# A four-layer kernel: layer 3's keys made inside the attention, its weights prepared in front of layer 2's end, three-step turns in layer 2, another order of sums and taps in layer 1

## Chip, cores and metric

The kernel runs on one core of a Trainium2 chip. The metric is device time in microseconds; lower is better. Engines are named as in the profile: PE (TensorE), PEld (its weight loads), DVE (VectorE), ACT (ScalarE), POOL (GpSimd), SP (SyncE, which issues all DMAs here).

## What is computed

The input x is 2x128x64x64 in float32 (2 batches, 128 channels, 4096 pixels). Four layers follow one another, each as a residual around a group norm:

```python
def _gn(v, G=32, eps=1e-5):           # mean and variance over groups of 4 channels
    ...
x = x + _L0_conv_ref(_gn(x), ...)     # 1x1 and 3x3 depthwise convolutions, two attentions over tokens and channels
x = x + _L1_conv_ref(_gn(x), ...)     # 1x3 convolution, correlations over shifts, 5x5 dilated depthwise taps
x = x + _L2_conv_ref(_gn(x), ...)     # rfft2, a quaternion product with weights per frequency, irfft2
x = x + _L3_conv_ref(_gn(x), ...)     # attention, 8 heads of 16 channels, 4096 queries and keys
```

In layer 3, q, k and v are 1x1 projections with a bias, the logits are divided by the root of 128, and softmax runs over all 4096 keys.

## The kernel before, in words

The whole x lies in SBUF as `X` (128 channels by 2 batches by 4096) and every layer adds to it in place. All loops are unrolled. Each layer is recorded under `_in_order`, which fixes every engine's order to the order of the program, so an instruction that waits holds what was written after it on its engine. DMAs are issued by SP in program order too. Pools of SBUF are opened and closed by layer, so a later layer's first load waits until the layer before has released its space.

*Layer 0* (`_layer0`): per batch `convolutions`, then `attention`, whose exps are ACT's L1294, scores PE's L1285, and products L1698. Before it, `_weights_by_rows` issues 136 DMAs (L764, L766) that rearrange layer 2's weights from HBM to HBM.

*Layer 1* (`_layer1`): loads its weights (L536 to L544); `padded` normalizes (L149); `columns_and_convolved` makes a convolution `t2` (L610) and transposed columns (L620); `correlated` multiplies columns (L635) and swaps the result (`swapped`, L646). Then come 42 taps of batch 0 on DVE (`taps`, L655), the matrices `t9` (`weights`, L693), and a loop over 2 batches and 8 chunks of 512 pixels (`NCH`). In each step, `on_tiles` (L674, for chunks 0 and 2, copied to `z` by ACT at L684) and `combined` (L703, 14 matmul instructions) run on PE; some taps of batch 1, a step of the next layer's statistics (`_stats_steps`: L1323, L1326, matmuls L1329 and L1338) and `added` (L714) run on DVE.

*Layer 2* (`_layer2`): first the transforms over h, 8 turns for each batch. `columns` normalizes on ACT (`g`, L832), transposes on PE (L839) and copies on DVE (`gt`, L845); `transformed` multiplies (L852) and copies on ACT (`y`, L853). `_skewed` runs `columns(i)` and then `transformed(i-1)`. Then come 8 blocks `kb` of two halves each. A half is `products` (L970) with weights loaded at L795, and beside it a chain of side steps, dealt out by `alongside`: `rows_in` transforms the rows of the next block (L874, ACT's L880, L887) and copies them into operands `e` (ACT's L910, DVE's L912); `turned` and `back` transform the results back (L999, L1006, L1024, L1027). In block 0 the first half also makes the mirrored operand of its own rows. At the end `turned_back` (L1091, L1099) and `added` (L1106, L1108) add to `X`.

*Layer 3* (`_layer3`): loads constants, weights and biases with 13 DMA issues (L104, L1870, L1874, L1876, L1878), prepares them (`weights`, L1887 to L1893), and folds the norm into them (`folded`, L1904 to L1923). `queries_and_keys` makes a batch's q and k in 8 chunks: a matmul (L1938), two shuffles on DVE (L1941, L1943), three scalings on ACT if `idle` (L1946 to L1948) or else on DVE, and two combinations on DVE (L1953, L1954). `values` makes `vt` in 8 groups (L1964, L1971). Both take their PSUM tiles from `acc`, which has two buffers; `attend` holds one of them as its accumulator. For each of 8 blocks `qb` and 32 tiles `kt`, `attend` makes scores (L2010), two exps (L2020) and, two tiles later, the products with `vt` (L2029). There are four such passes (2 batches, 2 halves of the heads). For the first pass, all 8 chunks and 2 groups of values are made ahead of it, and the other 6 groups inside it, one every third `kt`:

```python
                if kt % 3 == 0:
                    over = next(early, early) is early
```

For later passes all of this is side work of the pass before, one step at `kt` 4, 12 and 20, once `early` is over.

Of the kernel before, what the change touches and what calls it, by code (L numbers as in the profile page):

```python
# [520 lines left out]
def _layer1(ctx, tc, X, a, cst, here=None, there=None):  # L521
# [204 lines left out]
    rest = taps(1, g[1])  # L726
    steps = iter(())
    for b in range(B):
        for c in range(NCH):
            if c in (0, 2):  # L730
                z = on_tiles(g[b], t2[b], c // 2)
                some(rest, 4)
            ps = combined(t9[b], t2[b], c)
            some(rest, 2)
            some(steps, 2)
            added(b, c * CH, ps)
            if c in (1, 3):
                added(b, c // 2 * S // 2, z)
        if there is not None and b == 0:
            steps = _stats_steps(nc, two, bank, X[:, 0, :], cst, mhalf, there)  # L740


# [31 lines left out]
@with_exitstack  # L774
def _layer2(ctx, tc, X, weights, cst, src, here=None, there=None):

# [25 lines left out]
    with tc.tile_pool(name="l2_a", bufs=3) as ap, tc.tile_pool(  # L802
# [18 lines left out]
        for b in range(B):  # L821
# [7 lines left out]

            def columns(i):  # L830
                g = ap.tile([128, 8, H], F32, name="g")
                nc.scalar.activation(  # L832
                    g, xw[:, 8 * i : 8 * i + 8, :], AF.Identity, bias=shift, scale=scale
                )
                for _ in range(2):
                    next(steps, None)
                pt = aps.tile([128, CH], F32, tag="pt", name="ps_pt")
                for n in range(4):
                    nc.tensor.transpose(  # L839
                        pt[:, n * 128 : (n + 1) * 128],  # L840
                        g[:, 2 * n : 2 * n + 2, :].rearrange("p w h -> p (w h)"),
                        ident,
                    )
                gt = ap.tile([128, CH], F32, name="gt")
                nc.vector.tensor_copy(gt, pt)  # L845
                return gt
# [9 lines left out]

            _skewed(columns, transformed, W // 8)

    two = ctx.enter_context(tc.tile_pool(name="l2_two", bufs=2))
    with tc.tile_pool(name="l2_e", bufs=4) as ep, tc.tile_pool(  # L860
# [191 lines left out]
        for i in (0, 2):  # L1052
            for _ in rows_in(0, first[i : i + 2], (0,), es):
                pass
        before = None
        for kb in range(BLOCKS2):
# [7 lines left out]
            if before:  # L1064
                side += [turned(pzs[1], before[1]), back(kb - 1, *before)]
                n += 6
            else:
                side = [rows_in(0, first[i : i + 2], (1,), e) for i in (0, 2)] + side
                n += 10
            alongside(products(rows_of_weights(kb, False), e[0], pzs[0]), chain(*side), n)  # L1070
            side, n = [turned(pzs[0], direct)], 4
            if nxt:
                side = [rows_in(kb + 1, nxt[2:], (1, 0), es)] + side
                n += 8
            alongside(products(rows_of_weights(kb, True), e[1], pzs[1]), chain(*side), n)
            before = (direct, image)
        for _ in chain(turned(pzs[1], before[1]), back(BLOCKS2 - 1, *before)):
            pass


    with tc.tile_pool(name="l2_c", bufs=3) as cp, tc.tile_pool(
# [176 lines left out]
def _in_order(tc):  # L1258
# [4 lines left out]
    for i in block[start:]:  # L1263
        if i.engine in ENGINES:
            if i.engine in last:
# [7 lines left out]
                )  # L1273
            last[i.engine] = i.name


# [74 lines left out]
def _layer0(ctx, tc, X, a, cst, worst, there, dram):  # L1351
# [442 lines left out]
    for b in range(1, B):  # L1794
        _input(nc, X, a, b)
    rows_of_weights = _weights_by_rows(nc, dram, a)
    with _in_order(tc):
# [27 lines left out]
    for b in range(B):  # L1825
        w2 = small.tile([128, 128], F32, tag="w2", name="w2")
        with tc.tile_pool(name="f0_conv", bufs=1) as pool, _in_order(tc):
            ss2, own = convolutions(pool, b, before)
        side = [channel_attention(ss2, own, w2)]
        if b + 1 < B:  # L1830
# [7 lines left out]


@with_exitstack  # L1840
def _layer3(ctx, tc, X, a, cst, src, out, worst, here):
    nc = tc.nc
    SCALE = 1.0 / math.sqrt(C)
    OF_Q = [i % 16 for i in range(32)]
# [10 lines left out]

    k3 = _load_consts(nc, one, src, 2)

    upper, sign = k3["upper"], k3["sign"]
    lower = one.tile([128, 1], F32, name="lower")
    mhalf = one.tile([128, 1], F32, name="mhalf")  # L1860
    nc.vector.memset(mhalf, -0.5)
    head_sum = _all_ones_blocks(nc, one)


    w_qk = one.tile([128, 2, 4, 2, 16], F32, name="w_qk")
    b_qk = one.tile([128, 2], F32, name="b_qk")
    loaded = []
    for n, p in enumerate("qk"):
        w = two.tile([128, CH], F32, tag="ur"[n], name="w", bufs=1)[:, : 2 * 128]
        nc.sync.dma_start(w, a[f"L3_conv_w{p}"].rearrange("p t m -> p (t m)"))  # L1870
        loaded.append(w.rearrange("p (t j s i) -> p t j s i", t=2, s=2, i=16))
        for j in range(4):
            r = 32 * j + 16 * n
            nc.sync.dma_start(b_qk[r : r + 16, :], a[f"L3_conv_b{p}"][32 * j : 32 * j + 16, :])  # L1874
    w_v = one.tile([128, 192], F32, name="w_v")
    nc.sync.dma_start(w_v, a["L3_conv_wv"])  # L1876
    b_v = one.tile([128, 192], F32, name="b_v")
    nc.sync.dma_start(b_v, a["L3_conv_bv"].to_broadcast([128, 192]))  # L1878

    residual = [one.tile([128, CH], F32, name=f"residual{i}") for i in range(2)]  # L1880
    for r in residual:
        nc.gpsimd.memset(r, 0.0)

    def weights():
        for n, w in enumerate(loaded):
            for t in range(2):
                nc.vector.tensor_scalar_mul(  # L1887
                    w_qk[:, t, :, n, :], w[:, t, :, 0, :], SCALE if n == 0 else 1.0
                )
        nc.vector.tensor_scalar(lower, upper, -1.0, 1.0, ALU.mult, ALU.add)  # L1890
        scales = one.tile([128, 1], F32, name="scales")
        nc.vector.scalar_tensor_tensor(scales, lower, SCALE, upper, ALU.mult, ALU.add)
        nc.vector.tensor_scalar_mul(b_qk, b_qk, scales)  # L1893

# [32 lines left out]
    def queries_and_keys(b, t, f, q, k, idle):  # L1927
# [7 lines left out]
        for c in range(NCH):  # L1935
# [8 lines left out]
            hi = two.tile([128, CH], F32R, tag="hi", name="hi", bufs=1)  # L1944
            if idle:
                nc.scalar.activation(hi, kk, AF.Identity, bias=bk)  # L1946
# [55 lines left out]
    def attend(b, t, q, k, vt, early):  # L2002
# [58 lines left out]
        for qb in range(NCH):  # L2061
            for kt in range(NQT):
                if kt % 3 == 0:
                    over = next(early, early) is early
                waiting.append((qb, kt, scores(qb, kt)))
                if len(waiting) > 2:
                    multiply(*waiting.pop(0))
                yield kt if over else None
        for x in waiting:
            multiply(*x)  # L2070

    def work():

        for b in range(B):
            f = []
            yield from folded(b, f)
            for t in range(2):
# [4 lines left out]
                early = values(b, t, f, vt)  # L2082
                for n, _ in enumerate(early):
                    yield
                    if first and n == 1:
                        break
                yield from queries_and_keys(b, t, f, q, k, first)
                yield b, t, (q, k, vt, early)
# [9 lines left out]
    side = work()  # L2098

    next(side)  # L2100
    weights()
    found = []
# [45 lines left out]
def kernel(ctx, tc, a, out):  # L2148
# [4 lines left out]
    with tc.tile_pool(name="keep", bufs=1) as keep:  # L2153
# [4 lines left out]
        rows_of_weights = _layer0(tc, X, a, cst, worst, st[:, :B], dram)  # L2158
        _layer1(tc, X, a, cst, st[:, :B], st[:, B])
        _layer2(tc, X, rows_of_weights, cst, a["consts1"], st[:, B], st[:, B + 1])  # L2160
        _layer3(tc, X, a, cst, a["consts2"], out, worst, st[:, B + 1])
        with tc.tile_pool(name="flag_ps", bufs=1, space=PSUM) as fp:
# [68 lines left out]
```

## Time and profile before

| | |
|---|---|
| time, median of 3 runs | 4331.19 us (4329.97 to 4339.18) |
| the profiled execution's own time | 4336.11 us |
| its span, first to last instruction | 4334.3 us |
| PE, ACT, DVE, POOL busy | 94%, 77%, 50%, 2% of the span |
| granted PE clock, mean | 0.972 |
| layer 0, layer 1, layer 2, layer 3 | 0 to 1707.9, to 1965.7, to 2318.1, to 4334.3 us |

Most of the time is attention: layer 0's exps (L1294) occupy ACT for 992.5 us, layer 3's (L2020) for 1885.1 us. A busy PE in the profile isn't a PE at its peak, since the ends of matmuls are modelled. The stages between the attentions are shorter, and in each of them another engine or wait decides; they have to be read from their own windows. The profiled execution lies 4.9 us above the median.

### The profile page before, as it was taken

How to read it: one execution, taken by the hardware profiler on the slowest of the kernel's cores; microseconds unless marked ns; L12 is line 12 of the kernel's file. 1: busy time of each engine (PE TensorE's matmuls, PEld its weight loads, DVE VectorE, ACT ScalarE, POOL GpSimd, SP SyncE). 2: the span in 40 equal slices, each digit the busy share in tenths (PEclk: the TensorE clock that was granted, in tenths of full speed). 3: DMA queues.
4: the chain of work that ended last, by engine and by line, in shares of the span. 5: the costliest groups of instructions: out<-in, count | busy, mean ns of one | idle time of the engine just before them, and what ended most of it. 6: DMA issues, size and time to landing. Idle time of an engine off the chain costs nothing. (4 is left out here: it accounts for less than half of the span.)

```text
span 4334.3 us, 82274 instructions
## 1 busy us (share of the span) xinstructions
PE 4080.3 (94%) x35790; PEld 1559.5 (36%) x35790; DVE 2178.7 (50%) x2340; ACT 3353.9 (77%) x4069; POOL 67.5 (2%) x145
## 2 busy tenths in 40 slices
PE   6899999978999997996896999999999999999998
PEld 3432222245222224444664333333333333333332
DVE  3578999846999998994764112312122112211111
ACT  4378888734888884225553999999999999999998
POOL 1001000000000001000000000000000000000000
PEclk9999999989999999998997999999999999999999
DMA  9998000000000000002660000000000000000000
GB/s 206 187 182 115 1 1 1 1 1 2 1 1 1 1 1 7 1 1 114 260 273 8 4 6 6 6 4 6 6 6 4 6 6 6 4 6 6 6 6 4
DMA packets 158822, 158.86 MB, mean 37 GB/s; under 512 B 24809, under 2 KB 148713, under 8 KB 154354
## 3 DMA queue, kind: packets, MB, share of 16 engines
q1 hardware_dynamic: 158450, 153.50, 15.1%
q8 instruction: 282, 4.62, 0.4%
q14 instruction: 90, 0.74, 0.1%
HBM read 145.09 MB, written 73.40 MB: 50 GB/s over the span
## 5 line engine op out<-in xcount | busy, mean ns | idle before, releaser
L2020 ACT ACTIVATE weights<-ps_s 128x1024 f32<-128x1024 f32 x2048 | 1885.1, 1104 | 67.3 <-PE ps_s L2010 66.9
L1294 ACT ACTIVATE weights<-ps_s 128x1024 f32<-128x1024 f32 x1024 | 992.5, 1022 | 174.0 <-PE ps_s L1285 149.1
L2029 PE MATMUL ps_acc<-weights,vt 128*32 128x512 f32 x8192 | 1098.2, 608 | 0.0
L2010 PE MATMUL ps_s<-q,k 32*128 32x512 f32 x8192 | 929.4, 446 | 8.9 <-ACT weights L2020 8.9
L1733 DVE TENSOR_TENSOR sums<-sums,weights 128x2048 f32<-128x2048 f32 x384 | 879.0, 2289 | 42.1 <-ACT weights L1294 6.2
L2010 PEld LDWEIGHTS ps_s<-q,k 32*128 32x128 f32 x8192 | 474.8, 184 | 846.8 <-ACT weights L2020 785.1
L1285 PE MATMUL ps_s<-q,k 32*128 32x512 f32 x4096 | 645.8, 641 | 3.6 <-ACT weights L1294 2.2
L2051 DVE COPY u<-ps_acc 128x512 f32<-128x512 f32 x32 | 22.1, 691 | 1068.6 <-PE ps_acc L2029 1068.6
L1698 PE MATMUL ps_acc<-weights,vt 128*32 128x512 f32 x4096 | 548.9, 605 | 3.4 <-ACT used L1723 3.2
L1285 PEld LDWEIGHTS ps_s<-q,k 32*128 32x128 f32 x4096 | 209.6, 183 | 429.8 <-issue 212.5
L2029 PEld LDWEIGHTS ps_acc<-weights,vt 128*32 128x32 f32 x8192 | 163.4, 108 | 379.7 <-issue 367.8
L1698 PEld LDWEIGHTS ps_acc<-weights,vt 128*32 128x32 f32 x4096 | 81.0, 108 | 395.8 <-issue 377.7
L655 DVE SCALAR_TENSOR_TENSOR X<-g,w,X 128x2048 f32<-128x2048 f32 x84 | 197.3, 2350 | 2.4
L1489 PE MATMUL ps_sp<-pad,diag 32*32 32x512 f32 x4608 | 178.9, 633 | 9.8 <-DVE q L1500 5.5
L1733 DVE TENSOR_TENSOR sums<-weights 128x2048 f32<-128x2048 f32 x64 | 146.5, 2289 | 61.5 <-ACT weights L1294 61.5
L1971 DVE TENSOR_TENSOR vt<-ps_acc,bv 128x384 f32<-128x384 f32 x32 | 17.8, 557 | 294.3 <-PE ps_acc L1964 294.3
L970 PE MATMUL ps_z<-w_ri,e 128*32 128x128 f32 x2048 | 137.6, 408 | 8.8 <-DVE e L912 6.6
L1489 PEld LDWEIGHTS ps_sp<-pad,diag 32*32 32x32 f32 x4608 | 96.9, 106 | 79.5 <-issue 33.7
L1467 PE MATMUL ps_sp<-xn,w_qkv 128*128 128x512 f32 x160 | 88.6, 691 | 32.4 <-DVE k L1500 15.0
L2054 DVE RECIPROCAL r<-r 128x512 f32<-128x512 f32 x32 | 107.3, 3353 | 1.1
L912 DVE TENSOR_SCALAR e<-ps_pe 32x136 f32<-32x136 f32 (+1 forms) x352 | 104.4, 297 | 5.0
L910 ACT ACTIVATE e<-ps_pe 32x136 f32<-32x136 f32 (+1 forms) x352 | 99.2, 282 | 4.1
(285 smaller groups left out, 2514.1 us busy)
## 6 DMA issues: line engine op xcount, KB each, us to landing
w_ri<-w_r SPq DMA_DIRECT2D x16, 2112.0 KB, 8.2
w_ri<-w_i SPq DMA_DIRECT2D x16, 2112.0 KB, 13.4
w_r<-in_L_conv_kr_w SPq DMA_DIRECT2D x15, 528.0 KB, 13.1
w_r<-in_L_conv_kr_x SPq DMA_DIRECT2D x15, 528.0 KB, 12.8
w_r<-in_L_conv_kr_y SPq DMA_DIRECT2D x15, 528.0 KB, 12.7
w_r<-in_L_conv_kr_z SPq DMA_DIRECT2D x15, 528.0 KB, 12.6
w_i<-in_L_conv_ki_w SPq DMA_DIRECT2D x15, 528.0 KB, 12.7
w_i<-in_L_conv_ki_x SPq DMA_DIRECT2D x15, 528.0 KB, 12.1
```

Of the source, the lines that this page charges most:

```text
L655: nc.vector.scalar_tensor_tensor(xi, g[:, i : i + H // 2, j : j + W], w8[:, s : s + 1], xi, ALU.mult, ALU.add)
L912: nc.vector.tensor_scalar_mul(out, got[of, :, s], sign)
L970: nc.tensor.matmul(out.rearrange("p (n f o) -> p n f o", n=2, f=2), e[:, s, 2 * j : 2 * j + 2, :].rearrange("p f x -> p (f x)"), w.rearran ...
L1285: nc.tensor.matmul(ps[j // 2][:, j % 2, :], k[rows, kt * 128 : (kt + 1) * 128], q[rows, qb * CH : (qb + 1) * CH], start=True, stop=True,)
L1294: nc.scalar.activation(w[:, 2 * p : 2 * p + 2, :], ps[p], AF.Exp)
L1489: nc.tensor.matmul(ps[r // 2][to, r % 2, :].rearrange("p (h w) -> p h w", w=W), diag[rows, grp, t, :], pad[rows, y0 : y0 + ROWS, t % 3 : t ...
L1698: nc.tensor.matmul(ac[n][rows, :], lhs(rows), w[:, j, :], start=first, stop=last)
L1733: nc.vector.tensor_add(parts[0].rearrange("p j c -> p (j c)"), t.rearrange("p j c -> p (j c)"), w.rearrange("p j c -> p (j c)"),)
L2010: nc.tensor.matmul(ps[j // 2][:, j % 2, :], k[rows, kt * 128 : (kt + 1) * 128], q[n][rows, qb * CH : (qb + 1) * CH], start=(n == 0), stop= ...
L2020: nc.scalar.activation(w[p], ps[p], AF.Exp)
L2029: nc.tensor.matmul(ac[0][32 * j : 32 * j + 32, :], vt[:, kt, j // 2, i : i + 2, :].rearrange("p a d -> p (a d)"), w[j // 2][:, i, :], star ...
L2054: nc.vector.reciprocal(r, r)
```

## The change

Layer 3: the loads and the preparation of weights become functions of their own. The loads are issued ahead of layer 1, into two new pools; the preparation runs on DVE ahead of the last part of layer 2. The first pass begins after two chunks of keys (scaled on ACT) and two groups of values; the other six of each are made inside the pass, in turn, one every second `kt`, with the keys' scalings on DVE. Layer 2: the transforms over h take three steps per turn, with `transformed` two turns behind the normalization; in block 0, the rows of block 1 move from the first half to the second. Layer 1: a chunk's sum is written after the next chunk's `combined` and ahead of its taps, and the taps are dealt out 4 and 3 per step instead of 6 and 2. Layer 0: the DMAs of `_weights_by_rows` wait for the last instruction of batch 0's convolutions.

```diff
@@ _layer1
             if c in (0, 2):
                 z = on_tiles(g[b], t2[b], c // 2)
-                some(rest, 4)
             ps = combined(t9[b], t2[b], c)
-            some(rest, 2)
+            for x in ready:
+                added(*x)
+            ready = [(b, c * CH, ps)]
+            if c in (1, 3):
+                ready.append((b, c // 2 * S // 2, z))
+            some(rest, 4 if c in (0, 2) else 3)
             some(steps, 2)
-            added(b, c * CH, ps)
-            if c in (1, 3):
-                added(b, c // 2 * S // 2, z)
...
@@ _layer2
-            _skewed(columns, transformed, W // 8)
+            gs, gts = {}, {}
+            for i in range(W // 8 + 2):
+                if i < W // 8:
+                    gs[i] = normalized(i)
+                if 1 <= i <= W // 8:
+                    gts[i - 1] = columns(i - 1, gs.pop(i - 1))
+                if i >= 2:
+                    transformed(i - 2, gts.pop(i - 2))
...
             else:
-                side = [rows_in(0, first[i : i + 2], (1,), e) for i in (0, 2)] + side
-                n += 10
+                later = side
+                side, n = [rows_in(0, first[i : i + 2], (1,), e) for i in (0, 2)], 10
...
             if nxt:
-                side = [rows_in(kb + 1, nxt[2:], (1, 0), es)] + side
-                n += 8
+                side = later + [rows_in(kb + 1, nxt[2:], (1, 0), es)] + side
+                n += 8 + 8 * len(later)
+                later = []
...
+    if beside:
+        beside()
...
@@ _layer0
-    rows_of_weights = _weights_by_rows(nc, dram, a)
...
+        if b == 0:
+
+            with _after(tc):
+                rows_of_weights = _weights_by_rows(nc, dram, a)
...
@@ _layer3
-            if idle:
+            if c < idle:
                 nc.scalar.activation(hi, kk, AF.Identity, bias=bk)
...
-                if kt % 3 == 0:
+                if kt % 2 == 0:
                     over = next(early, early) is early
...
-                for n, _ in enumerate(early):
-                    yield
-                    if first and n == 1:
-                        break
-                yield from queries_and_keys(b, t, f, q, k, first)
+                keys = queries_and_keys(b, t, f, q, k, 2 * first)
+                if first:
+
+                    for _ in range(2):
+                        next(keys)
+                        next(early)
+                        yield
+                    early = in_turn(keys, early)
+                else:
+                    for _ in early:
+                        yield
+                    yield from keys
...
@@ tile_conv_preact_kernel
-        _layer1(tc, X, a, cst, st[:, :B], st[:, B])
...
+        with tc.tile_pool(name="late", bufs=1) as late:
+            with tc.tile_pool(name="raw", bufs=1) as raw:
+                l3 = _layer3_inputs(nc, late, raw, a, a["consts2"])
+                _layer1(tc, X, a, cst, st[:, :B], st[:, B])
+                _layer2(
...
+                    lambda: _layer3_weights(nc, l3),
+                )
+            _layer3(tc, X, l3, cst, out, worst, st[:, B + 1])
```

The new functions: `_after` gives every instruction recorded under it a wait for the last instruction recorded before; `_layer3_inputs` issues the 13 loads that layer 3 issued itself, and `_layer3_weights` holds the seven DVE operations of its former `weights`; `in_turn` takes one step of each generator by turns.

## The prediction

> **What bounds the kernel now.** I read the trace by stage first, because shares over the whole span mix stages with different limits. The stage borders are the places in the timeline where one layer's last instruction and the next layer's first stand. Columns: window and length, then busy time (instruction count) of PE, PE's weight loads, DVE, ACT, POOL, the granted PE clock, DMA share, GB/s.
>
> ```profile
> 0.00:1707.90 1707.90, 1582.90 (x14347) 551.70 (x14347) 1344.10 (x1061) 1188.65 (x1365) 54.46 (x115) 0.98 0.26 45
> 1707.90:1965.70 257.80, 243.51 (x1546) 113.79 (x1546) 236.09 (x166) 71.75 (x114) 9.74 (x21) 0.96 0.01 3
> 1965.70:2020.90 55.20, 28.86 (x196) 25.30 (x196) 16.84 (x31) 27.85 (x32) 0.55 (x1) 0.91 0.40 167
> 2020.90:2290.80 269.90, 235.33 (x2776) 159.51 (x2776) 180.91 (x496) 153.45 (x469) 0.00 (x0) 0.91 0.57 226
> 2318.10:2366.80 48.70, 22.44 (x56) 11.21 (x56) 25.22 (x68) 17.09 (x25) 1.32 (x5) 0.59 0.07 17
> 2366.80:4334.30 1967.50, 1944.29 (x16673) 676.02 (x16673) 359.08 (x494) 1885.11 (x2049) 0.55 (x1) 0.99 0.02 5
> ```
>
> See two rows where no engine is half busy or little more: layer 2's transforms over h (55.2 us) and layer 3's front (48.7 us). They are chains of waits. Layer 1 (257.8 us) is full on PE and DVE both; layer 3's attention is full on PE and ACT.
>
> The timelines of those places come next. Columns: start, duration, engine, line, names, count, and in brackets the idle time before and its releaser. Layer 1 (SP, PE, PE, DVE, PE):
>
> ```profile
> 1707.86 0.34 SPq L536 DMA_DIRECT2D w<-in_L_conv_w  x1
> ...
> 1710.70 5.46 PE L610 MATMUL ps_bank<-g,w 128*128 128x512 f32 x6 [3.70 <-DMA w<-in_L_conv_w]
> 1818.91 0.55 PE L646 MATMUL ps_bank<-consts,raw 128*128 128x128 f32 x3 [0.57 <-ACT raw L643]
> ...
> 1823.18 14.28 DVE L655 SCALAR_TENSOR_TENSOR X<-g,w,X 128x2048 f32<-128x2048 f32 x6
> ...
> 1943.45 0.56 PE L1329 MATMUL ps_bank<-gn_mv,consts 128*128 128x1 f32 x2 [9.47 <-DVE gn_mv L1326]
> ```
>
> PE's first work waits for a load; from there to L646 it runs almost unbroken. From 1823 to 1943 DVE has no gap, then PE waits for it, and three more `combined` (18.6 us) end the layer. Layer 2's transforms over h and the start of its products (ACT, ACT, PE):
>
> ```profile
> 1979.19 1.25 ACT L832 ACTIVATE g<-X,shift,st 128x512 f32<-128x512 f32 x1
> 1982.09 0.59 ACT L853 COPY y<-ps_py 128x512 f32<-128x512 f32 x1 [1.64 <-PE ps_py L852]
> ...
> 2063.45 1.27 PE L887 MATMUL ps_pe<-consts,yt 128*128 128x136 f32 x4 [7.20 <-ACT e L910]
> ```
>
> ACT idles 1.64 us in every turn; a turn lasts 3.37 us (the next L832 is at 1982.57). In block 0 PE stands 7.2 us once. Layer 3's front and first attention steps (DVE, then ACT):
>
> ```profile
> 2320.82 0.30 DVE L1887 TENSOR_SCALAR w_qk<-w 128x64 f32<-128x64 f32 x2 [2.65 <-DMA b_qk<-in_L_conv_bq]
> ...
> 2334.56 0.75 DVE L1953 SCALAR_TENSOR_TENSOR k<-hi,consts,kk 128x512 fp32r<-128x512 f32 x1 [1.84 <-ACT kk L1947]
> ...
> 2366.78 5.77 ACT L2020 ACTIVATE weights<-ps_s 128x1024 f32<-128x1024 f32 x6
> ...
> 2396.49 5.60 ACT L2020 ACTIVATE weights<-ps_s 128x1024 f32<-128x1024 f32 x6 [0.85 <-PE ps_s L2010]
> 2402.95 67.94 ACT L2020 ACTIVATE weights<-ps_s 128x1024 f32<-128x1024 f32 x74 [0.86 <-PE ps_s L2010]
> ```
>
> The first exp stands behind all eight chunks of keys. Undisturbed, 74 exps take 67.94 us, or 1.836 us per `kt`; each group of values put in between costs ACT 0.86 us.
>
> **What the Trainium skill says.** "PSUM — Partial Sum Buffer", section "Engine vs sequencer instructions": ACT and DVE queues are strict FIFO and matmuls keep program order. The trace agrees: the next L832 needs nothing late, yet starts only behind L853. "DMA: Bandwidth & Descriptors", section "Anatomy of one DMA": a DMA's semaphore wait is taken on the issuing sequencer before dispatch, so what stands behind it in SP's queue waits too. Layer 1's loads do stand behind their first wait until 1707.86. "TensorE: Matmul & The Clock Gate", section "What's actually happening": PE runs at half clock after about 3.4 us of idleness. The six L610 above take 5.46 us, later sixes 2.76.
>
> **Layer 0: -3 us.** The copies of layer 2's weights (136 DMA issues, 13 to some 390 us, DMA share about 1) now wait for the end of batch 0's convolutions and run beside its attention, from 226 to some 560 us. SP has nothing else to issue until 1707. The convolutions gain little: the same PE stretch up to the first L1285 takes 65.4 us under the copies (160.84 to 226.23) and 63.5 without (1000.82 to 1064.34); with the earlier part I take 3. The attention should lose nothing: at 260 to 300 us, under the copies, PE did 7.6 matmuls per us, at 500 to 700 7.5. Bounds -6 and +4.
>
> **Layer 1: +9 us.** *Loads.* Layer 3's 13 DMA issues now stand in SP's queue in front of layer 1's five, behind the same wait. In the trace they last from 2317.53 to 2323.63, 6.1 us. So L536 goes out at 1714.0 instead of 1707.86, PE starts at 1716.8 instead of 1710.7, and L646 ends at about 1825.6. DVE isn't held by its own loads (needed at 1717.3 to 1718, there at about 1716.5 to 1717.3), finishes `taps(0)` as now, and then waits for the second `swapped`, from 1821.2 to 1825.6: +4.4.
> *Sums.* In DVE's order the sums keep their places between the taps; only the counts change, from 6 and 2 taps per step to 4 and 3. Today six taps (14.2 us) cover `on_tiles` and the first `combined` on PE (8.7+6.2). Four (9.4) don't: DVE reaches the first sum at 1836.9, PE at 1840.4, +3.5, and +1.0 at the third. All 42 taps still come ahead of the statistics, so the tail after 1943 stays. Sum 8.9; bounds +5 (the gaps are slack) and +11 (6.1 in full).
>
> **Layer 2, transforms: -20 us.** With three-step turns, a turn's L853 needs a matmul whose `gt` was made one turn earlier. A turn is then ACT's own work: 1.16 (two L832 took 2.41, one 1.25) plus 0.49. In the first four turns DVE needs 1.8 (two L1323 and an L845). Stepping the three engines through these durations gives 51.3 us for the order before (measured 55) and 32.6 for the new one; scaled, 35. Bounds: -22, and -12 if PE stays at half clock (2.6 us a turn).
>
> **Layer 2, block 0: -9 us.** The 7.2 us wait is L887's for a buffer that ACT frees only after both copies of the row before; in the changed kernel's order this instruction waits for its own copy and a DVE one done earlier. That is -7.2, and some 2 us as `rows_in(1)` leaves the first half, where four pairs of copies (about 3.6 us each on ACT and DVE) stand against 6.2 us of products, for the second. Bounds -12 and -2 (the wait returns elsewhere). Weights for a half arrive 15 us after its issue, about a half's length, so DMA stays beside it.
>
> **Layer 3: -32 us.** *Front.* The weights' operations (about 1.3 us) move into DVE's gap of 8.7 us at 2285.5. L1904 then starts at 2318.1, not 2324.32. One chunk takes 4.54 us (36.3 for eight). After: 3.2 us to the first shuffle, chunk 0 4.6, its values 0.6, and 3.7 until ACT has done chunk 1. First exp at 2330.2 instead of 2366.78: -36.6.
> *Attention.* Six chunks and six groups of values now lie in it instead of six groups. Before, 15 `kt` took 36.2 us (2366.78 to 2402.95) against 27.5 undisturbed: 8.6 lost. Twelve items lose some 4.5 at the start and ten times 0.87: 13.2, +4.6. A chunk off ACT is 4.2 us of DVE, values 0.6, per 7.3 us of attention, so DVE keeps up; chunk c is asked for eight `kt` ahead. One later step of side work slips by one turn, beside the attention: 0. Bounds -34 and -24.
>
> **Sum.** -3+9-20-9-32 = -55. The profiled execution took 4336.1 us, so 4281 on its terms; it stands 4.9 above the median 4331.2, which gives **4276**.
>
> **Rivals.** *Turns don't pay (0.15):* PE's clock stays low in layer 2's turns (8 us less gained) and the 7.2 us come back (7 less): 4276+15 = 4291. For it: the clock is 0.91 there; against: PE will idle less. *Moved copies hurt (0.05):* instruction fetch shares the DMA engines, and the attention loses 5% of 330 us: 4292; the count at 260 to 300 us speaks against. *Keys too late (0.09):* all twelve items share the one PSUM buffer that the accumulator leaves free, and PE stands still from a chunk's matmul until DVE has read it. At the longest wait of L1938 today, 3.6 us per item, 12 times 2.7 us more: 4309. From 0.87+55/12 = 5.5 us per item the kernel is slower; at 6, if DVE's whole chunk and PE's matmul lie in series, 4338. Against: values alone cost 0.86.
> The likeliest case (0.71) is the sum. Its bounds give 4262 (-69) to 4308 (-23); both ends at once are unlikely, so 4262 to 4303 with the first two rivals inside. About 0.2% (9 us) is what a measurement of this kernel tells from no change. Slower is the third rival's far end and what I overlook.
>
> **What would show it.** L536 issued 6 us after layer 0's last POOL operation; DVE idle before L693 and the first sum; turns of 1.7 us; no 7 us before L905 (today's L887); the first exp of layer 3 some 60 us earlier than today (36.6+20+9+3-9); then ACT gaps near 0.9 us. Wrong: gaps of 3 us and more there, or an attention of batch 0 below 7.5 matmuls per us.

## The result, and the profile after

The changed kernel takes 4273.11 us (median of 4 runs, 4264.27 to 4279.18) against 4332.65 us (4 runs, 4329.97 to 4339.18): a ratio of 0.9859, 95% interval 0.9837 to 0.9880. Two later comparisons, in which the changed kernel ran again beside experiments, gave 0.9834 (0.9816 to 0.9852) and 0.9834 (0.9816 to 0.9851). So it is faster by 60 to 72 us. The profiled execution of the changed kernel was the fastest of its four (4264.27 us, span 4262.5), so sums over the two traces come out larger than the first ratio.

The trace after, by the same stages as before (window and length; busy time and count of PE, PE's weight loads, DVE, ACT, POOL; granted clock, DMA share, GB/s):

```profile
0.00:1693.50 1693.50, 1573.87 (x14347) 551.67 (x14347) 1343.87 (x1060) 1188.31 (x1365) 54.63 (x114) 0.98 0.26 45
1693.50:1959.80 266.30, 242.78 (x1546) 113.49 (x1546) 236.22 (x166) 71.55 (x114) 10.06 (x21) 0.95 0.02 5
1959.80:1994.20 34.40, 28.23 (x197) 25.50 (x197) 16.52 (x30) 27.72 (x32) 0.55 (x1) 0.90 0.64 268
1994.20:2261.70 267.50, 233.69 (x2777) 156.69 (x2777) 181.87 (x503) 154.04 (x470) 0.00 (x0) 0.92 0.58 228
2288.20:2300.40 12.20, 8.33 (x38) 4.68 (x38) 7.82 (x26) 4.29 (x6) 1.59 (x5) 0.86 0.11 24
2300.40:4262.50 1962.10, 1940.24 (x16693) 673.54 (x16691) 383.22 (x547) 1884.81 (x2048) 0.55 (x1) 1.00 0.02 5
```

Read the lengths against those before. Layer 0: 1707.9 to 1693.5. Layer 1: 257.8 to 266.3. Transforms over h: 55.2 to 34.4. Layer 2's blocks: 269.9 to 267.5. Layer 3's front: 48.7 to 12.2. Its attention: 1967.5 to 1962.1. The two thin rows of the table before, the transforms and layer 3's front, shrank most, and ACT is busy 27.72 of 34.40 us in the third row.

Layer 1 after, in the timelines of SP and DVE (start, duration, engine, line, names, count, idle time before and releaser):

```profile
1693.52 0.34 SPq L104 DMA_DIRECT2D consts<-in_consts  x1
...
1699.51 0.43 SPq L536 DMA_DIRECT2D w<-in_L_conv_w  x1
```

```profile
1810.96 0.87 DVE L693 SCALAR_TENSOR_TENSOR t<-ps_bank,p,p 128x128 f32<-128x128 f32 x3 [3.72 <-PE ps_bank L646]
...
1812.97 9.50 DVE L655 SCALAR_TENSOR_TENSOR X<-g,w,X 128x2048 f32<-128x2048 f32 x4
1825.92 0.69 DVE L714 TENSOR_TENSOR X<-ps_bank,X 128x512 f32<-128x512 f32 x1 [3.44 <-PE ps_bank L703]
```

L536, layer 1's own first load, stands 6 us behind the first of layer 3's loads, DVE idles 3.72 us ahead of L693, and four taps (9.50 us) don't cover PE's work, so DVE idles 3.44 us more ahead of the first sum.

A turn of the transforms on ACT:

```profile
1969.17 1.28 ACT L840 ACTIVATE g<-X,shift,st 128x512 f32<-128x512 f32 x1
1970.35 0.58 ACT L864 COPY y<-ps_py 128x512 f32<-128x512 f32 x1
1970.82 1.29 ACT L840 ACTIVATE g<-X,shift,st 128x512 f32<-128x512 f32 x1
```

No bracket stands behind L864 any more: ACT waits for nothing, and this turn is 1.65 us long, not 3.37. (Most turns take 1.64 to 1.87 us; the third of each batch, at half the granted clock, takes 3.3 to 3.4.) Block 0 on PE:

```profile
2023.84 0.64 PE L988 MATMUL ps_z<-w_ri,e 128*32 128x128 f32 x8 [4.38 <-DVE e L930]
...
2034.56 0.73 PE L905 MATMUL ps_pe<-consts,yt 128*128 128x136 f32 x4 [1.84 <-ACT yt L898]
...
2043.17 0.63 PE L1017 MATMUL ps_bank<-consts,pz 128*66 128x128 f32 x4 [2.43 <-ACT pzt L1024]
...
2045.94 0.64 PE L988 MATMUL ps_z<-w_ri,e 128*32 128x128 f32 x2 [1.58 <-DVE e L930]
```

The single wait of 7.20 us is gone, and four smaller ones stand in its place; the longest holds the whole second half until the copies into the mirrored operand, called image copies below, are made. The first exps of layer 3 on ACT:

```profile
2300.41 7.44 ACT L2070 ACTIVATE weights<-ps_s 128x1024 f32<-128x1024 f32 x8 [1.10 <-PE ps_s L2060]
2308.69 3.77 ACT L2070 ACTIVATE weights<-ps_s 128x1024 f32<-128x1024 f32 x4 [0.85 <-PE ps_s L2060]
2313.32 3.77 ACT L2070 ACTIVATE weights<-ps_s 128x1024 f32<-128x1024 f32 x4 [0.85 <-PE ps_s L2060]
```

They begin 66 us sooner than before (2366.78). For the twelve items (six chunks of keys and six groups of values) ten gaps of 0.85 us follow, so two of the items leave none. The gaps of 3.44 and 1.01 us that the kernel before had among its first exps are absent.

### The profile page after: what moved, and what is told of

It is laid out like the page before. It is cut to its first block, busy times and chain, and to the rows that moved or that the text cites. A ratio compares the mean times of both kernels' runs of the same rounds, so it can differ in the third digit from the quotient of the medians.

```text
span 4262.5 us, 82256 instructions
## 1 busy us (share of the span) xinstructions
PE 4050.0 (95%) x35790; PEld 1547.6 (36%) x35790; DVE 2185.9 (51%) x2358; ACT 3340.0 (78%) x4051; POOL 68.3 (2%) x145
## 3 DMA queue, kind: packets, MB, share of 16 engines
q8 instruction: 282, 4.62, 0.4%
## 5 line engine op out<-in xcount | busy, mean ns | idle before, releaser
L1330 ACT ACTIVATE weights<-ps_s 128x1024 f32<-128x1024 f32 x1024 | 992.5, 1022 | 173.2 <-PE ps_s L1321 148.2
L1769 DVE TENSOR_TENSOR sums<-sums,weights 128x2048 f32<-128x2048 f32 x384 | 879.0, 2289 | 42.2 <-ACT weights L1330 6.2
L1525 PE MATMUL ps_sp<-pad,diag 32*32 32x512 f32 x4608 | 166.9, 607 | 3.8 <-DVE q L1536 2.3
L1503 PE MATMUL ps_sp<-xn,w_qkv 128*128 128x512 f32 x160 | 92.9, 719 | 33.7 <-DVE k L1536 16.2
## 6 DMA issues: line engine op xcount, KB each, us to landing
w_r<-in_L_conv_kr_y SPq DMA_DIRECT2D x15, 528.0 KB, 12.2
```

What stands on the lines that cost most here:

```text
L1330: nc.scalar.activation(w[:, 2 * p : 2 * p + 2, :], ps[p], AF.Exp)
L1525: nc.tensor.matmul(ps[r // 2][to, r % 2, :].rearrange("p (h w) -> p h w", w=W), diag[rows, grp, t, :], pad[rows, y0 : y0 + ROWS, t % 3 : t ...
L1769: nc.vector.tensor_add(parts[0].rearrange("p j c -> p (j c)"), t.rearrange("p j c -> p (j c)"), w.rearrange("p j c -> p (j c)"),)
```

## Experiments

My theory after these traces was: each part works where the prediction put it, but the moved copies are worth three times what I took, block 0 a fifth, and the attention doesn't pay for the keys. Times and ratios (to the kernel before, run beside them):

| kernel | median us (runs) | ratio, 95% interval |
|---|---|---|
| copies in front | 4280.40 (6) | 0.9873, 0.9854 to 0.9892 |
| loads behind | 4276.47 (5) | 0.9843, 0.9819 to 0.9866 |
| loads behind, taps 6/2 | 4259.11 (5) | 0.9817, 0.9800 to 0.9834 |
| two-step turns | 4291.43 (6) | 0.9894, 0.9878 to 0.9911 |
| keys in front | 4299.85 (6) | 0.9903, 0.9886 to 0.9920 |
| block 0 as before | 4269.35 (5) | 0.9840, 0.9821 to 0.9859 |
| a quarter of the copies in front | 4277.08 (5) | 0.9855, 0.9834 to 0.9875 |
| changed kernel, again | 4268.95 (5) | 0.9834, 0.9816 to 0.9852 |
| copies at batch 1 | 4297.59 (5) | 0.9878, 0.9855 to 0.9901 |
| one chunk of keys in front | 4260.99 (5) | 0.9819, 0.9801 to 0.9837 |
| loads behind, taps 6/2, again | 4259.53 (5) | 0.9814, 0.9792 to 0.9836 |
| changed kernel, third time | 4272.87 (5) | 0.9834, 0.9816 to 0.9851 |

The first four ran together, the next four, and the last four. Runs of one kernel lie up to 24 us apart, so I take sizes from the stage concerned in the traces and use the ratios as a control. Most kernels have one trace, so a difference in a stage is firmest where several traces share that stage's code.

### Copies in front

```
         _input(nc, X, a, b)
+    rows_of_weights = _weights_by_rows(nc, dram, a)
...
-        if b == 0:
-
-            with _after(tc):
-                rows_of_weights = _weights_by_rows(nc, dram, a)
```

> The changed kernel with the copies of layer 2's weights issued in front again, as in the kernel before. Theory (the copies slow batch 0's convolutions): +11 to +14 us on the changed kernel, all of it in layer 0. The depthwise groups (L1525 in the changed kernel) take some 13 us each while the DMA row is full, against 9.7 us; the first scores start near 226 us, not 215; layer 0 ends 11 to 14 us later. Rival (the copies cost what the prediction took, and the rest of layer 0's gain came with the one profiled execution): +2 to +6 us, and first scores not over 220 us.

From batch 0's first L1503 to the first scores it takes 185.3 us; ten profiles of kernels with the changed layer 0 have 170.7 to 173.2, the kernel before 181.7. Layer 0 ends at 1709.3 us; in those ten at 1693.5 to 1700.6 (mean 1697.7), before at 1707.9. So the gain in layer 0 is 10 us on average, not the 14 of the one profile, and it goes when the copies return. The ratio stands 0.0014 to 0.0039 above those of the changed kernel, or 6 to 17 us. The rival (+2 to +6, first scores by 220 us) falls: they start at 230.0 us. The depthwise groups did not take 13 us each, as expected, but 9.8 to 16.0. PE's timeline in the kernel before shows two of its stops and a slow group:

```profile
63.18 2.12 PE L1489 MATMUL ps_sp<-pad,diag 32*32 32x512 f32 x37 [1.28 <-issue]
...
135.89 2.29 PE L1489 MATMUL ps_sp<-pad,diag 32*32 32x512 f32 x58 [0.69 <-issue]
...
147.63 13.28 PE L1489 MATMUL ps_sp<-pad,diag 32*32 32x512 f32 x288
```

and in the changed kernel:

```profile
142.05 9.72 PE L1525 MATMUL ps_sp<-pad,diag 32*32 32x512 f32 x284 [0.80 <-DVE q L1536]
...
155.50 9.76 PE L1525 MATMUL ps_sp<-pad,diag 32*32 32x512 f32 x288
```

Before, PE stops four times with no releaser ("issue"), 2.9 us in all, and its 2304 depthwise matmuls of batch 0 are busy for 93.0 us. After, there is no such stop, and they take 82.2 to 84.9 us in the ten profiles. The slow group shown, of 13.28 us, is another matter: the granted clock in it is 0.80.

### A quarter of the copies in front

```
+    rows_of_weights = _weights_by_rows(nc, dram, a, range(BLOCKS2 // 4))
...
+                rows_of_weights |= _weights_by_rows(nc, dram, a, range(BLOCKS2 // 4, BLOCKS2))
```

> The changed kernel with the first quarter of the copies of layer 2's weights in front and three quarters behind batch 0's convolutions. Theory (PE's small matmuls are slowed only while the copies run): the load on the DMA engines ends near 115 us; PE's waits for nothing (issue) in the depthwise groups and groups longer than 10.5 us stand only ahead of that, and the first scores come at 219 to 222 us, between the 215 to 218 without copies and the 226 to 230 with them; +3 to +5 us. Rival (what differs is the clock granted, whatever the DMA engines do): long groups and issue waits spread over all of the stretch, or none at all; first scores at 215 to 218.

PE's timeline, batch 0's convolutions:

```profile
64.87 3.86 PE L1525 MATMUL ps_sp<-pad,diag 32*32 32x512 f32 x37 [2.82 <-issue]
...
92.00 3.81 PE L1525 MATMUL ps_sp<-pad,diag 32*32 32x512 f32 x100 [1.07 <-issue]
...
112.49 5.40 PE L1525 MATMUL ps_sp<-pad,diag 32*32 32x512 f32 x143 [0.72 <-issue]
...
127.31 12.99 PE L1525 MATMUL ps_sp<-pad,diag 32*32 32x512 f32 x288
```

The DMA share falls from 1.2 to 0.56 in the stretch 100 to 120 us and to 0.01 behind it; the last copy's packet lands at 112.3 us. The third stop ends at 112.49 us, and no stop comes after it, in one and the same instruction stream: the stops belong to the copies. The size was missed: first scores at 224.5 us, not 219 to 222. The last line is a slow group where no copy runs; the changed kernel, run again, has one too (13.02 us). The granted clock is 0.80 in the one and 0.79 in the other. So slow groups alone are no sign of the copies.

### Copies at batch 1

```
-        if b == 0:
-
-            with _after(tc):
-                rows_of_weights = _weights_by_rows(nc, dram, a)
...
             attention(pool, chain(*side))
+        if b == 0:
+            with _after(tc):
+                rows_of_weights = _weights_by_rows(nc, dram, a)
         before = finish(b, w2)
```

> The changed kernel with the copies of layer 2's weights begun at the end of batch 0's attention, so that they run beside batch 1's convolutions (832 to 1004 us of the changed kernel). Theory (a stream of small matmuls is held up while the DMA engines are full, wherever it stands): batch 1's convolutions, 172 us in the changed kernel's runs, take 177 to 184, with PE waits for nothing (issue) in the depthwise groups, which batch 0 then doesn't have; +5 to +11 us on the changed kernel. Rival (batch 0's stretch is sensitive because it stands at the kernel's start): batch 1's convolutions 172 us, the time within 3 us of the changed kernel.

Batch 0's stretch takes 172.1 us, as without copies. Batch 1's first six groups, up to L1585, take 188.0 us instead of some 172, and the next stretch, with two more groups, 50.6 instead of 46.5: 20 us in all. The ratio is 0.9878 against 0.9834, some 19 us. It is more than expected, and the rival falls: the loss isn't bound to the kernel's start. PE's timeline there:

```profile
949.91 4.49 PE L1525 MATMUL ps_sp<-pad,diag 32*32 32x512 f32 x130
955.38 4.48 PE L1525 MATMUL ps_sp<-pad,diag 32*32 32x512 f32 x128 [0.98 <-issue]
962.15 1.15 PE L1525 MATMUL ps_sp<-pad,diag 32*32 32x512 f32 x30 [2.30 <-issue]
```

Between the two stops lie exactly 128 matmuls, with their 128 weight loads: 256 instructions. The Trainium skill, "Runtime: NRT & Kernel Launch", section "Instruction fetch mechanics", says that an engine's instructions are fetched in blocks of 16 KiB, 256 instructions, by a DMA queue of its own, and calls the cost of a border "mostly hidden". The queue table of this run's profile agrees on the block:

```profile
q8 instruction: 282, 4.62, 0.4%
```

(packets, MB, share of 16 engines): 4.62 MB over 282 packets is 16.4 KB, and 282 blocks of 256 are just enough for PE's 35790 matmuls and as many weight loads. Two counts in the traces tie the stops to these blocks. Counted through PE's instructions from the kernel's first, all 21 stops without a releaser in the four traces with copies beside convolutions stand at place 192 or 193 of a run of 256. And each of them ends 1.3 to 2.1 us after the packet of its own block has landed. The ten traces of kernels with the changed layer 0 have no such stop in their convolutions.

So the fetch is not hidden here. PE goes through a block in 4.5 us of depthwise matmuls, and while the copies fill the DMA engines the next block comes up to 2.3 us late in these lines, 3.9 us at most in this trace. The stops alone add up to 15.6 us. The step from the last matmul of one block to the first of the next is longer than a stop, since the last matmul's modelled 0.6 us cover its beginning: in batch 1's depthwise groups these steps, where over 0.2 us, add up to 18.9 us, against 0.8 to 1.0 in five traces without copies there. That is nearly all of the 20 us. Whether the DMA engines or the memory behind them hold a packet up isn't shown.

The attention, at 7.0 to 7.5 matmuls and as many weight loads per us, takes 17 to 18 us for a block, and has no such stop. Its stretch, from the first scores to batch 1's convolutions, is 617.3 to 621.0 us long with the copies in it, and 620.7 in this run, which has none there.

### Loads behind, and taps 6 and 2

```
     nc.sync.dma_start(p9.rearrange("p k c -> p (k c)"), a["L1_conv_p9w"].to_broadcast([128, 7 * C]))
+    for to, x in loads:
+        nc.sync.dma_start(to, x)
...
-            some(rest, 4 if c in (0, 2) else 3)
+            some(rest, 6 if c in (0, 2) else 2)
```

The first kernel has the loads alone, the second both; the second ran again later. In all of them `_layer3_inputs` collects its transfers in a list, passed on as `loads`, instead of issuing them.

> The changed kernel with layer 3's 13 loads issued behind layer 1's five loads instead of ahead of them. Theory (layer 1's first loads are late by the issues that stand in front of them): -4 to -6 us, with layer 1's first load issued within 1 us of layer 0's end, and layer 3's start no later, since its weights are prepared 550 us after. Rival (layer 1's start waits for its normalization, and the loads are hidden by it): 0, within 1 us.

> The changed kernel with layer 3's loads behind layer 1's, and the taps of layer 1 at 6 and 2 for each chunk instead of 4 and 3; the sums stay ahead of the taps. Theory (the 4/3 taps cost 3.5 us, since they leave more of them behind the last chunk): -8 to -9 us on the changed kernel, the tail behind the last combination shorter. Rival (the taps are hidden beside TensorE's chunks, what counts is the sums' place): the same as with the loads alone, -4 to -6 us. Third (the longer turn of six taps makes a bank late, and TensorE waits for it again): -1 to -4 us, with waits for ps_bank of 3 us or more.

> The kernel with loads behind layer 1's and taps 6 and 2 once more, beside the changed kernel on one chip. Theory (5.2 us of loads and 3.5 of taps, as its trace had them): -7 to -10 us on the changed kernel. Rival (the first comparison was spread): within 3 us of it.

Layer 1 (from layer 0's end to the first L840 or its like) takes 266.3 us in the changed kernel and 266.1 to 266.3 in its two repeats, 261.1 with the loads behind, 257.6 and 258.3 with both, 258.0 before. So the loads cost 5.2 us and the taps' counts 2.8 to 3.5; the new place of the sums costs nothing. DVE in the second run with both, where six taps cover PE and no sum waits:

```profile
1811.41 14.28 DVE L657 SCALAR_TENSOR_TENSOR X<-g,w,X 128x2048 f32<-128x2048 f32 x6
1825.61 0.68 DVE L716 TENSOR_TENSOR X<-ps_bank,X 128x512 f32<-128x512 f32 x1
```

This version is faster than the kernel before by some 81 us (ratio 0.9814), and its median lies below the changed kernel's too: 4259.53 us beside 4272.87. There the ratios differ by only 0.0020, or 9 us, with intervals that overlap; the stage shows 8. The rivals fall by the stage: the loads aren't hidden by the normalization, the taps' counts do matter, and no bank comes late. By its ratio (0.9843) the kernel with the loads alone shows no gain; 5 us are less than the spread of its runs.

### Two-step turns

```
-            gs, gts = {}, {}
-            for i in range(W // 8 + 2):
...
+            _skewed(lambda i: columns(i, normalized(i)), transformed, W // 8)
```

> The changed kernel with layer 2's transforms over h in turns of two steps as before (normalization, transposes and copy of one part in one step). Theory (the turn is set by the chain normalization, transposes, copy, and the three-step turn takes the first link off it): +20 us, all in layer 2's transforms, turns of 2.8 us instead of 1.7. Rival (the gain came from layer 1's end and from the first part's loads, not from the turns): +0 to +8 us.

From the first L840 to the first product 69.8 us instead of 42.2: +27.6; before it was 62.9. The rival falls. The excess of 7 over the expected 20 is in batch 0's turns, 4.64 us each, where 2.8 were expected and the kernel before had 3.37 after the first. The stretches of the two batches (columns as in the first fence):

```profile
1962.70:1996.00 33.30, 21.04 (x95) 19.41 (x96) 11.09 (x22) 13.15 (x15) 0.55 (x1) 0.54 0.67 276
1996.00:2024.00 28.00, 14.61 (x102) 12.67 (x101) 5.53 (x8) 14.15 (x18) 0.00 (x0) 0.94 0.00 1
```

In the first the granted clock is 0.54: half clock lasts 30.7 us. The kernel before has the same two-step turns with the same waits, was back at full clock after 6.8 us, and has 0.91 over its transforms, as the three-step turns have 0.90. So the order of the steps is worth the 20 us; the other 7 are half clock that these turns may or may not meet, and what decides it isn't shown.

### Block 0 as before

```
-                later = side
-                side, n = [rows_in(0, first[i : i + 2], (1,), e) for i in (0, 2)], 10
+                side = [rows_in(0, first[i : i + 2], (1,), e) for i in (0, 2)] + side
+                n += 10
...
-                side = later + [rows_in(kb + 1, nxt[2:], (1, 0), es)] + side
-                n += 8 + 8 * len(later)
-                later = []
+                side = [rows_in(kb + 1, nxt[2:], (1, 0), es)] + side
+                n += 8
```

> The changed kernel with block 0 of layer 2 in the order of the kernel before: the spectra of block 1's first rows are made in the first half again. Theory from the two traces (the 7.2 us wait comes back, but the new waits of 4.4, 5.0 and 1.8 us behind the image copies go): +1 to +3 us on the changed kernel, all between the first product and block 1's. Rival (the prediction's sum): +7 to +11 us.

PE's timeline has the old wait back to the hundredth:

```profile
2041.78 1.27 PE L905 MATMUL ps_pe<-consts,yt 128*128 128x136 f32 x4 [7.20 <-ACT e L928]
```

Yet block 0, from its first product to the seventh matmul of block 1 (behind the last of the four new waits), takes 45.9 us instead of 44.5 in the changed kernel's run beside it, and the ratio is that of the changed kernel. The new order is worth 1.4 us here and 1.9 between the first two traces; up to block 1's first matmul it is 2.3 and 2.6. The old wait went, and one of 3.27 us ahead of it (2053.95 us in the kernel before), but the new ones take most of that back: between block 0's first eight matmuls and block 1's first, PE's waits are 11.7 us before and 9.5 after.

### Keys in front, and one chunk in front

```
-                keys = queries_and_keys(b, t, f, q, k, 2 * first)
+                keys = queries_and_keys(b, t, f, q, k, 8 * first)
...
-                        next(keys)
                         next(early)
                         yield
-                    early = in_turn(keys, early)
+                    yield from keys
```

> The changed kernel with all eight chunks of layer 3's first keys made ahead of the attention again, on ACT; two groups of values ahead too, the other six inside the attention, one to two kt. The weights stay ready in front. Theory (six chunks cost 4.54 us each in front and under 1 us each inside the attention): front +27 to +30, attention -4 to -6, together +22 to +26 us on the changed kernel. Rival (an item inside the attention costs 3 us or more, as the prediction's third rival had it): the move had paid little, +5 to +12 us. Rival (the front was set by the loads, not by the keys): +0 to +8 us.

From the first L1988 to the first exp 37.3 us instead of 10.7: +26.7, 4.4 per chunk. The first 24 `kt` of the attention take 51.1 us against 53.6: six keys cost 2.5 us inside. By ratio the whole is some 30 us; these two places hold 24 of them. The rest seems to lie behind the first 32 `kt`, which take 1899.3 us against 1893.2 to 1897.4 in the traces with the keys inside; why isn't shown. Both rivals fall. The first 24 `kt` gained only half of what was expected from taking the keys out. The stretch at its start tells why; keys in front, then the changed kernel (columns as in the first fence):

```profile
2304.70:2342.00 37.30, 17.51 (x36) 6.19 (x35) 21.77 (x48) 17.02 (x24) 0.00 (x0) 0.59 0.02 5
2342.00:2352.00 10.00, 8.88 (x50) 4.16 (x51) 2.02 (x4) 7.35 (x9) 0.00 (x0) 0.56 0.00 0
```

```profile
2300.40:2310.00 9.60, 8.81 (x72) 3.63 (x72) 6.65 (x17) 8.75 (x10) 0.00 (x0) 1.00 0.00 0
```

After a long front in which PE is busy for less than half the time the attention starts at a clock of 0.56, as it did in the kernel before (also 0.56 from 2366.8 to 2380), with 50 matmuls in 10 us. After the short front it starts at 1.00 here, with 72 in 9.6. The Trainium skill, "TensorE: Matmul & The Clock Gate", section "What's actually happening", has the half clock after an idle window of about 3.4 us. In the long front the clock was halved after a stop of PE of 3.61 us, which agrees; but in the changed kernel it was halved, for 3.4 us just ahead of the first exp, after one of 2.59 us, so the length of the last stop alone doesn't tell.

> Candidate: loads behind layer 1's, taps 6 and 2, and only one chunk of layer 3's keys and one group of values ahead of the attention instead of two. Theory (a chunk costs some 4 us in front and about 0.4 to 0.9 inside): first exp 3 to 5 us sooner after the last sum of layer 2, 26 kt long then as in the other, -2 to -3 us against loads behind and taps 6/2 alone. Rival (chunk 1 comes too late for the fifth kt, and each later item with it): a gap of 2 us or more before an exp among the first ten kt, 0 to +5 us.

The edit takes the range of that loop from 2 to 1, and `2 * first` to `1 * first`, on top of loads behind and taps 6/2. It is a miss: 4260.99 us beside 4259.53 without it. The front is 4.4 us shorter (6.7 instead of 11.0), but gaps before the first exps are back (ACT):

```profile
2297.38 1.94 ACT L2075 ACTIVATE weights<-ps_s 128x1024 f32<-128x1024 f32 x2 [1.57 <-PE ps_s L2065]
2300.05 1.94 ACT L2075 ACTIVATE weights<-ps_s 128x1024 f32<-128x1024 f32 x2 [0.73 <-PE ps_s L2065]
```

The clock is 0.66 in its first 10 us of attention. The first 32 `kt` take 72.7 us instead of 68.2, and what the front gave is gone. No gap reaches the rival's 2 us. But the slow start isn't shown to come from the shorter front: the first run of loads behind and taps 6/2 has two chunks in front, over 10.5 us, and starts in the same way, at a clock of 0.63:

```profile
2314.39 1.94 ACT L2075 ACTIVATE weights<-ps_s 128x1024 f32<-128x1024 f32 x2 [1.57 <-PE ps_s L2065]
2317.06 1.94 ACT L2075 ACTIVATE weights<-ps_s 128x1024 f32<-128x1024 f32 x2 [0.72 <-PE ps_s L2065]
```

Its first 32 `kt` take 70.8 us. So of the 4.5 us that this run lost, 2.6 go with such a start and 1.9 with its two further items inside the attention.

### The changed kernel again

> The changed kernel, nothing edited, to have its time and a second trace beside the other three. All theories: 4264 to 4280 us; layer 0 ends at 1693 to 1701 us, as in the runs that share its layer 0; first scores at 215 to 218 us.

> The changed kernel, nothing edited, beside the other three. All theories: 4264 to 4280 us; batch 1's convolutions 172 us.

Medians of 4268.95 and 4272.87 us, and the stages as given above.

## Why the prediction was right, and where it was not

The prediction was right: 4276 us against 4273.11, faster. By its own steps:

- **Layer 0, -3: mis-sized.** Measured -10 (ten profiles against the one before). The step that failed is "with the earlier part I take 3". I measured 1.9 us on the last 65 us of batch 0's stretch and took 1 for the other 116. To the same point (the eight L1467 at 160.84, the eight L1503 at 151.70) those took 116.3 us before and 107.2 after: 9.1 us. My second rival had the cause, instruction fetch, but put it on the attention. There it was rightly priced at nothing: the attention runs through its instructions four times more slowly. The sign of error that I gave for it, fewer than 7.5 matmuls per us, did come (7.0 from 226 to 560 us), but it was badly chosen: the run without copies there has 6.9 over the same stretch.
- **Layer 1, +9: right.** +8.3; loads 5.2 (4.4 predicted), taps 2.8 to 3.5 (4.5).
- **Transforms, -20: right.** -20.7 in the traces, and undone by the one edit.
- **Block 0, -9: mis-sized.** -1.9 to -2.6, at the edge of the bounds "-12 and -2". The -7.2 was right for the instruction and wrong for the path. The term that failed is "some 2 us as `rows_in(1)` leaves the first half". In the new order PE reaches the second half early and stands 4.38 us until the image copies, which I had counted myself as 3.6 us a pair, are done.
- **Layer 3's front, -36.6: right.** -36.5.
- **Attention, +4.6: mis-sized.** The term that failed is "some 4.5 at the start": it did not come back, since PE started at or near full clock in ten of eleven traces. The other ten items cost 0.85 us each (0.87 predicted). The first 24 `kt` take 53.5 to 53.6 us in ten of the eleven profiles with the changed attention (56.1 in one), against 52.6 before: +1.0. The whole attention takes 1961 to 1966 us in the eleven, 1963 on average, against 1967.5 in the one before. What is shorter behind the start is the granted clock's doing. Behind the first 32 `kt` the kernel before takes 1900.3 us, of which the granted clock withholds 15.3 (the length times what the mean clock lacks of 1); the eleven take 1893.2 to 1897.4, with 7.8 to 13.3 withheld. Without that share both are alike, 1885.0 and 1883.9 to 1885.7. Nothing in the change was meant to do this, and why the clock fell less often isn't shown.

With these sizes the sum is -10 + 8 - 21 - 2 - 36 + 1 = -60, and the rest of the attention adds -5: -65, between the first comparison's -59.5 and the later ones' -72. The total was nearer than its parts by luck: layer 0 and the attention together gave some 16 us more than I took, block 0 some 7 less. Of the rivals, the turns paid, the attention of batch 0 lost nothing, and the keys came in time.

Some readings behind the prediction were off without moving its sum. The three `combined` at layer 1's end take 21.0 us, not 18.6, since the first runs at half clock (8.57). ACT does not idle 1.64 us in every turn of the transforms; the first turns of a batch idle longer and last up to 4.65 us. And the copies' last issue is at 405 us before and at 601 after, not at some 390 and 560.

Both late blocks and the clock slow the depthwise groups of batch 0, and the traces tell them apart. In the kernel before, the steps between blocks add up to 6.7 us, against 0.6 to 0.8 in two traces of the changed kernel: that is 6 of the 10 us. Three of its eight groups run at a clock of 0.72 to 0.89 and are the longest, 13.3 to 15.5 us; the five others run at 1.00. The changed kernel's first trace has no slow group in batch 0, its second one at 0.79. What stays open is whether late blocks bring the low clock about.

## What to carry to other kernels

A bulk copy is not free merely because the DMA engines have nothing else to do: put it beside long instructions, not beside a stream of small matmuls, whose next instructions come through the same engines. A front or a turn in which PE idles can cost twice, by its length and by the half clock afterwards; look at the granted clock of the stage behind it, and in more than one trace, before you put a price on it. When a wait of one instruction is removed by a new order, add up what the same engines must finish before the next half, and book the gain against that, not against the wait.

## What the runs showed of the hardware that I had not expected

- While copies filled the DMA engines, PE stopped without a releaser at the borders of 256-instruction blocks: all 21 such stops in four traces stand there, each ending 1.3 to 2.1 us after its block had landed. They last up to 3.9 us, 15.6 us in all in the run with the copies at batch 1; the changed kernel's convolutions have none.
- The granted clock of the first 10 us of an attention can differ after the same front. After some 37 us with PE busy less than half the time it was 0.50 in the kernel before and 0.56 with the keys in front; after fronts of 10.5 to 11 us it was 0.97 to 1.00 in ten traces and 0.63 in one; after 6.7 us, in the only trace, 0.66.
